# Three of the first six layer-norm passes on GpSimd instead of VectorE, and the first two weight loads released two tiles earlier

## The chip, the cores and the metric

The kernel runs on one core of one Trainium2 chip. The metric is the device time of one execution in microseconds (us). It is given as the median of several executions, and one execution is also recorded by the hardware profiler.

## What is computed

The reference is a transformer block with global attention and relative position terms, followed by a spectral layer. Everything is float32; the image has 48 x 48 = 2304 tokens of 768 channels. Cut to what matters here:

```
xn  = layernorm(x, ln1_g, ln1_b)                 # over the 768 channels of each token
qkv = xn.reshape(2304, 768) @ qkv_w + qkv_b      # 768 -> 3 x 768
q, k, v = qkv split into 12 heads of 64
attn = softmax(q * scale @ k^T + rel_h + rel_w)
x = x + (attn @ v) @ proj_w + proj_b
x = x + gelu(layernorm(x) @ mlp_w1 + b1) @ mlp_w2 + b2
x = x + irfft2(softshrink(two block layers(rfft2(x))))   # layer 1
```

The change lies in the first line of this: the layer norm of the first 768 tokens, and the loads of the first columns of qkv_w.

## The kernel before

Tokens lie on the 128 partitions of the on-chip memory, so the 2304 tokens are 18 tiles of 128. Three tiles are a group (`arrive(g)` loads them into one buffer `x3`), and two groups are a block of 768 tokens. The first stage, `queries_keys_values`, has three such blocks (`p` = 0, 1, 2). In each block, six pairs of heads give queries and keys (`queries_and_keys`), and three calls of `values` give the values.

The matrix products of this stage use Strassen's scheme in Winograd's form: seven products of half size in the place of eight. It needs sums of blocks of both operands. The sums of the tokens are made on VectorE by `sums_of_tokens` (L171, four instructions of 128x1152). The sums of the weights are made on GpSimd by `left` (L153 to L156, four instructions of 128x384 for each pair of heads), as soon as that pair's weights have landed.

Before the first product, a tile passes through these steps:

1. `arrive` asks for the tile on SP's queue (L386).
2. `normalise` (L111 to L126): two `bn_stats` (L115) and one `bn_aggr` (L117) on VectorE give mean and variance; ScalarE takes the root (L119); VectorE takes the reciprocal (L120) and then writes (x - mean) * rstd in place with one `tensor_scalar` of 128x768 (L123).
3. `channels_first` (L395 to L411) transposes the group on TensorE (L401, 18 transposes a group, in PSUM banks m0 to m3 that are used in turn). VectorE (L404) and ScalarE (L408) write the transposed tiles, scaled and shifted, to `xt`, every second channel block each.

The order in the program is: tiles 0 to 5 normalised, group 0 transposed, group 1 transposed, sums of tokens, first pair of heads.

`weights_of(pr, slot, behind)` asks for the two halves of one pair's weights on SP's queue (L362, 384 KB each). For the first two pairs the load is made to wait for an instruction, `behind`: the list `normalised` holds the last instruction of each tile's `normalise`, and the two loads wait for those of tiles 2 and 4. Then `weights_of` calls `left` on GpSimd.

The order on TensorE and on SP's queue is the order of the program text (`manual_schedule`). The order on VectorE, ScalarE and GpSimd in this stage is set by the planner of the tile framework when the kernel is built: from the instructions that are ready by its own reckoning, it takes the one that stands first in the program. The hardware then runs each engine's list strictly in that order. The statistics `stats`, `mv` and `rstd` come from a pool with three buffers each, so tile 3 uses those of tile 0, and so on.

GpSimd has, besides the sums of the weights, the additions at L612, L679, L926, L1066, L1067, L1105 and L1270, and one `tensor_scalar` with constant operands late in the kernel (L1247).

Of the kernel before, what the change touches and what calls it, by code (L numbers as in the profile page):

```python
# [13 lines left out]
ALU = mybir.AluOpType  # L14
# [30 lines left out]
def block_then_afno(  # L45
# [26 lines left out]
    nc = tc.nc  # L72
# [35 lines left out]
    xt = shared[:, : NC * TB].rearrange("p (c t) -> p c t", c=NC)  # L108
    xs = shared[:, NC * TB :].rearrange("p (k c t) -> p k c t", k=3, c=3)

    def normalise(pool, src, hat=None, made=None):  # L111

        stats = pool.tile([P, 2, 6], F32, name="stats")
        for i in range(2):
            nc.vector.bn_stats(stats[:, i, :], src[:, ts(i, C // 2)])  # L115
        mv = pool.tile([P, 2], F32, name="mv")
        nc.vector.bn_aggr(mv, stats.rearrange("p a b -> p (a b)"))  # L117
        rstd = pool.tile([P, 1], F32, name="rstd")
        nc.scalar.activation(rstd, mv[:, 1:2], AF.Sqrt, bias=eps)  # L119
        nc.vector.reciprocal(rstd, rstd)  # L120
        if hat is None:
            hat = pool.tile([P, C], F32, name="hat", bufs=4)
        last = nc.vector.tensor_scalar(hat, src, mv[:, 0:1], rstd, ALU.subtract, ALU.mult)  # L123
        if made is not None:
            made.append(last)
        return hat  # L126
# [25 lines left out]
    def left(eng, a11, a12, a21, a22, s):  # L152
        eng.tensor_tensor(s[0], a21, a22, ALU.add)  # L153
        eng.tensor_tensor(s[1], s[0], a11, ALU.subtract)  # L154
        eng.tensor_tensor(s[2], a12, s[1], ALU.subtract)
        eng.tensor_tensor(a21, a11, a21, ALU.subtract)  # L156
# [30 lines left out]
    with ExitStack() as flag_scope:  # L187
# [11 lines left out]
        with ExitStack() as att:  # L199
# [120 lines left out]
            def queries_keys_values(qkv):  # L320
# [19 lines left out]
                ln1 = qkv.enter_context(tc.tile_pool(name="ln1", bufs=3))  # L340
# [18 lines left out]
                def weights_of(pr, slot, behind=None):  # L359
                    w, ws = pairs[slot]  # L360
                    for i in range(2):
                        load = nc.sync.dma_start(  # L362
                            out=w[:, :, i],
                            in_=qkv_w[:, ds(i * C + pr * P, P)].rearrange("(c p) f -> p c f", p=P),
                        )
                        if behind is not None:
                            tc.add_manual_dep(
                                load.ins, behind.ins.name,
                                mybir.DependencyInfo(
                                    mybir.DependencyClass.Sync, mybir.DependencyReason.DATA  # L370
                                ),
                                reason="tokens first",
                            )
                    left(
                        nc.gpsimd, w[:, 0:3, 0], w[:, 3:6, 0], w[:, 0:3, 1], w[:, 3:6, 1],
                        [ws[:, i] for i in range(3)],
                    )
                    return w, ws
# [10 lines left out]
                normalised = []  # L389

                def normal(t):
                    x3 = arrived[t // 3]
                    normalise(ln1, x3[:, t % 3], x3[:, t % 3], normalised)

                def channels_first(g):  # L395
                    x3 = arrived[g]
# [96 lines left out]
                for t in range(6):  # L493
                    normal(t)
# [7 lines left out]
                    orders.append(work)  # L502

                pairs_left = [i for work in orders for kind, i in work if kind == 0]
                ahead = [weights_of(pairs_left.pop(0), i, normalised[2 + 2 * i]) for i in range(2)]
                slot = 0
                for p in range(T // TB):
                    for g in (2 * p, 2 * p + 1):
                        channels_first(g)
                    sums_of_tokens(xt, xs)  # L510
                    for n, (kind, i) in enumerate(orders[p]):
                        if kind:
                            values(p, i)
                        else:
                            queries_and_keys(p, i, *ahead.pop(0))
                            if pairs_left:
                                ahead.append(weights_of(pairs_left.pop(0), slot % 2))
                                slot += 1

                        if p == 0 and n in (3, 4):  # L520
                            weights_of_values(n - 3)
                        elif (p, n) == (0, 5):
                            constants()
                        elif p < 2 and n in (1, 2):
                            arrive(2 * p + 1 + n)
                        if p < 2 and 2 <= n < 8:
                            normal(6 * p + 4 + n)
                        if p == 2 and n == 0:
                            fetch(0)
                        elif p == 2 and n in (1, 2, 3):  # L530
                            for j in (0, 1):
                                columns(0, 2 * (n - 1) + j)
                        elif p == 2 and n in (4, 6, 8):
                            relative(0, n // 2 - 2)
                        elif p == 2 and n == 5:
                            fetch_values(0)

            with tc.manual_schedule(engines={mybir.EngineType.PE, mybir.EngineType.SP}):
                with ExitStack() as qkv:
                    queries_keys_values(qkv)  # L540
# [78 lines left out]
                with tc.manual_schedule(engines={mybir.EngineType.Activation}):  # L619
                    for n, (pr, c, u) in enumerate(runs):  # L620
# [8 lines left out]
                        made = []  # L629
# [10 lines left out]
                        if pr < NC - 1:  # L640
                            if (c, u) in ((3, 1), (4, 0), (4, 1)):
                                i = 2 * (2 * (c - 3) + u - 1)
# [89 lines left out]
        with tc.If(safe < 1):  # L732
            with ExitStack() as att:
                xnT = main.rearrange("p (c t) -> p c t", c=NC)
                with tc.tile_pool(name="g_ln1", bufs=3) as ln1, tc.tile_pool(
                    name="g_ps_ln1", bufs=2, space=PSUM
                ) as psum:
                    for g in range(T // G):
                        hats = []
                        for i in range(3):  # L740
                            xi = ln1.tile([P, C], F32, name="g_xt")
                            nc.sync.dma_start(out=xi, in_=x[ts(3 * g + i, P), :])
                            hats.append(normalise(ln1, xi))
                        transposed(psum, hats, xnT, g, V_LN1G, V_LN1B, tag="m")
# [174 lines left out]
        with tc.tile_pool(name="ps_proj", bufs=2, space=PSUM) as psum:  # L919
            hats = []  # L920
            for t in range(EARLY, NT):
                projected(psum, t, later[t] if t in later else outputs(t))
                n = t - EARLY
                if n < 6:
                    hats.append(normalise(ln2, x1[:, n, :]))
                    nc.gpsimd.tensor_tensor(x1[:, n, :], x1[:, n, :], b2, ALU.add)  # L926
                if n in (2, 5):
                    transposed(psum, hats, xt, n // 3, V_LN2G, V_LN2B, tag="t")
                    hats = []
                if n == 5:  # L930
                    sums_of_tokens(xt, xs)
# [554 lines left out]
```

## Time and profile before

| | us |
|---|---|
| median of 3 runs | 2903.45 |
| lowest and highest | 2902.31 and 2904.82 |
| profiled execution, its own time | 2902.43 |
| span of the profiled execution | 2900.4 |
| TensorE busy in the span | 2848.4 (98%) |
| VectorE busy | 1789.9 (62%) |
| ScalarE busy | 936.2 (32%) |
| GpSimd busy | 612.4 (21%) |

The span runs from the first to the last instruction of the program; the time of the execution is 2.0 us longer. Times in the profile are counted from the start of the span. TensorE was granted 0.996 of its full clock on average. Of the span, the stage that the change touches is the start: the first transpose begins at 8.17 us, and the first product of weights and tokens at 20.08 us.

### The profile page before, as it was taken

How to read it: one execution, taken by the hardware profiler on the slowest of the kernel's cores; microseconds unless marked ns; L12 is line 12 of the kernel's file. 1: busy time of each engine (PE TensorE's matmuls, PEld its weight loads, DVE VectorE, ACT ScalarE, POOL GpSimd, SP SyncE). 2: the span in 40 equal slices, each digit the busy share in tenths (PEclk: the TensorE clock that was granted, in tenths of full speed). 3: DMA queues.
4: the chain of work that ended last, by engine and by line, in shares of the span. 5: the costliest groups of instructions: out<-in, count | busy, mean ns of one | idle time of the engine just before them, and what ended most of it. 6: DMA issues, size and time to landing. Idle time of an engine off the chain costs nothing. (4 is left out here: it accounts for less than half of the span.)

```text
span 2900.4 us, 41241 instructions
## 1 busy us (share of the span) xinstructions
PE 2848.4 (98%) x15803; PEld 1703.9 (59%) x15803; DVE 1789.9 (62%) x2606; ACT 936.2 (32%) x1514; POOL 612.4 (21%) x564
## 2 busy tenths in 40 slices
PE   8999999999999999999999999999999999999998
PEld 5555665555555555555555555555555555556884
DVE  5243237777777777777733666675666666666554
ACT  1011125656566565665500210122111211112341
POOL 3303010000000000000043323333332322222441
PEclk9999999999999999999999999999999999999999
DMA  4323376172552716435252111212221212123235
GB/s 154 129 98 104 108 157 124 29 135 59 87 125 43 145 34 103 109 58 87 57 180 77 49 55 55 66 58 75 64 66 49 93 55 66 45 63 109 77 99 182
DMA packets 204595, 255.59 MB, mean 88 GB/s; under 512 B 22050, under 2 KB 182754, under 8 KB 202854
## 3 DMA queue, kind: packets, MB, share of 16 engines
q1 hardware_dynamic: 201930, 249.18, 33.5%
q10 hardware_dynamic: 2460, 3.69, 0.4%
q8 instruction: 127, 2.08, 0.3%
q14 instruction: 78, 0.64, 0.1%
HBM read 136.88 MB, written 52.20 MB: 65 GB/s over the span
## 5 line engine op out<-in xcount | busy, mean ns | idle before, releaser
L635 DVE TENSOR_TENSOR acc<-acc,main 128x768 f32<-128x768 f32 x576 | 551.8, 958 | 206.4 <-ACT main L569 149.7
L569 ACT ACTIVATE main<-sp 128x768 f32<-128x768 f32 x648 | 520.8, 812 | 138.9 <-PE sp L565 132.3
L565 PE MATMUL sp<-terms,select 64*128 64x384 f32 x1296 | 413.3, 631 | 0.0
L1051 DVE TENSOR_TENSOR main<-o,main 128x384 f32<-128x384 f32 x540 | 299.1, 556 | 38.8 <-PE o L1049 0.3
L989 PE MATMUL h<-shared,w 128*128 128x384 f32 x864 | 296.6, 486 | 0.8 <-issue 0.8
L559 PE MATMUL sp<-shared 64*128 64x384 f32 x1296 | 268.0, 490 | 2.5 <-DVE o L455 2.2
L559 PE MATMUL sp<-qT,kT 64*128 64x384 f32 x1296 | 266.7, 487 | 0.2
L612 POOL TENSOR_TENSOR inverse<-inverse,rden 128x384 f32<-128x384 f32 x36 | 46.4, 1288 | 1013.5 <-DVE rden L609 944.8
L444 PE MATMUL m<-main 128*128 128x384 f32 x756 | 246.0, 487 | 3.8 <-DVE main L171 2.9
L989 PEld LDWEIGHTS h<-shared,w 128*128 128x128 f32 x864 | 163.9, 190 | 116.3 <-issue 2.6
L989 PE MATMUL h<-shared,w1s 128*128 128x384 f32 x648 | 226.6, 486 | 0.0
L582 PE MATMUL op<-main,shared 128*64 128x384 f32 x1296 | 221.2, 488 | 0.0
L582 PE MATMUL op<-main,v 128*64 128x384 f32 x1296 | 219.9, 488 | 0.0
L995 ACT ACTIVATE hT<-c,vec 128x384 f32<-128x384 f32 x108 | 66.4, 615 | 464.9 <-DVE c L1001 464.7
L444 PEld LDWEIGHTS m<-main 128*128 128x128 f32 x756 | 142.9, 190 | 104.3 <-issue 5.0
L1001 DVE TENSOR_TENSOR c<-h,u 128x384 f32<-128x384 f32 x108 | 60.2, 557 | 212.3 <-PE h L989 212.3
L1049 PE MATMUL o<-w2s,hs 128*128 128x384 f32 x432 | 174.9, 487 | 3.2 <-DVE hs L154 3.2
L1049 PE MATMUL o<-w,hT 128*128 128x384 f32 x432 | 175.0, 487 | 3.0 <-DVE mv L117 2.0
L565 PEld LDWEIGHTS sp<-terms,select 64*128 64x128 f32 x1296 | 125.8, 187 | 84.0 <-issue 0.5
L989 PEld LDWEIGHTS h<-shared,w1s 128*128 128x128 f32 x648 | 123.1, 190 | 85.9
L153 POOL TENSOR_TENSOR w1s<-w 128x384 f32<-128x384 f32 x36 | 36.9, 1024 | 601.8 <-PE o L1049 302.1
L559 PEld LDWEIGHTS sp<-shared 64*128 64x128 f32 x1296 | 117.7, 187 | 61.4 <-issue 22.8
(158 smaller groups left out, 3860.1 us busy)
## 6 DMA issues: line engine op xcount, KB each, us to landing
w<-in_mlp_w_dram SPq DMA_DIRECT2D x72, 768.0 KB, 4.4
terms<-col_parts SPq DMA_DIRECT2D x432, 72.0 KB, 3.0
terms<-row_hi SPq DMA_DIRECT2D x216, 72.0 KB, 2.8
terms<-row_lo SPq DMA_DIRECT2D x216, 72.0 KB, 3.0
main<-in_qkv_w_dram SPq DMA_DIRECT2D x36, 384.0 KB, 4.5
z<-zt SPq DMA_DIRECT2D x48, 192.0 KB, 1.9
x<-in_x_blocks_dram SPq DMA_DIRECT2D x18, 384.0 KB, 4.6
k_d<-o SPq DMA_DIRECT2D x36, 192.0 KB, 1.8
```

Of the source, the lines that this page charges most:

```text
L444: nc.tensor.matmul(bank, a[:, c, :], b[:, c, :], start=(first and c == 0), stop=(c == 2), skip_group_check=not first,)
L559: nc.tensor.matmul(sp[:, j, :G], kT[at, ts(kt, P)], qT[at, ts(c, G)], start=True, stop=False,)
L565: nc.tensor.matmul(sp[:, j, :G], select[at, a % 2], ready[pr, c][at, a // 2, b], start=False, stop=True,)
L569: nc.scalar.activation(p, sp[:, :, :G], AF.Exp, scale=HD**-0.5)
L582: nc.tensor.matmul(op[ts(j, 64)], v[:, kt0 + i, ts(j, 64)], ps[i][:, j, :], start=(kt0 + i == 0), stop=(kt0 + i == NT - 1),)
L612: nc.gpsimd.tensor_tensor(inverse, inverse, rden, ALU.add)
L635: nc.vector.tensor_tensor(acc, made[0] if kt == 1 else acc, p, ALU.add)
L989: nc.tensor.matmul(bank[i], a[:, c, :], b[:, c, :], start=(start and c == 0), stop=(c == 2), skip_group_check=not start,)
L995: nc.scalar.activation(h[:, i, ts(k, G)], src, AF.Gelu, bias=col(V_B1 + 2 * n + i))
L1001: nc.vector.tensor_tensor(t, src, other, ALU.add)
L1049: nc.tensor.matmul(bank[k], a, b, start=start, stop=True, skip_group_check=not start)
L1051: nc.vector.tensor_tensor(dst, bank[k], dst, ALU.add)
```

## The change

In `normalise`, the engine of the last instruction becomes a parameter. For tiles 1, 3 and 5 it is GpSimd, for all others VectorE as before; statistics, root and reciprocal stay where they were. The two first weight loads wait for the last instruction of tiles 0 and 2, both of which are VectorE's, in the place of tiles 2 and 4.

```diff
-    def normalise(pool, src, hat=None, made=None):
+    def normalise(pool, src, hat=None, made=None, engine=nc.vector):
...
-        last = nc.vector.tensor_scalar(hat, src, mv[:, 0:1], rstd, ALU.subtract, ALU.mult)
+        last = engine.tensor_scalar(hat, src, mv[:, 0:1], rstd, ALU.subtract, ALU.mult)
...
                 def normal(t):
                     x3 = arrived[t // 3]
-                    normalise(ln1, x3[:, t % 3], x3[:, t % 3], normalised)
+
+                    engine = nc.gpsimd if t in (1, 3, 5) else nc.vector
+                    normalise(ln1, x3[:, t % 3], x3[:, t % 3], normalised, engine)
...
-                ahead = [weights_of(pairs_left.pop(0), i, normalised[2 + 2 * i]) for i in range(2)]
+                ahead = [weights_of(pairs_left.pop(0), i, normalised[2 * i]) for i in range(2)]
```

## The prediction

> **What bounds the kernel now.** I read the busy shares first, since they say what a saving anywhere else is worth.
>
> ```profile
> PE 2848.4 (98%) x15803; PEld 1703.9 (59%) x15803; DVE 1789.9 (62%) x2606; ACT 936.2 (32%) x1514; POOL 612.4 (21%) x564
> ```
>
> TensorE (PE) is busy for 98% of the span. So a change at the start can only move the moment from which TensorE runs without a gap; everything behind it slides along. To find that moment I took the waits of the first 30 us and then the timeline of the first 60 us (start, duration, engine, line).
>
> ```profile
> POOL main L153 <- DMA main<-in_qkv_w_dram: 14.6, 2, 14.4
> PEld m L401 <- DVE x L123: 9.8, 4, 8.2
> ```
>
> ```profile
> 7.49 1.22 DVE L123 TENSOR_SCALAR x<-x,mv,rstd 128x768 f32<-128x768 f32 x2
> ...
> 9.84 5.69 SPq L362 DMA_DIRECT2D main<-in_qkv_w_dram  x4
> ...
> 14.80 1.00 POOL L153 TENSOR_TENSOR main<-main 128x384 f32<-128x384 f32 x1 [14.36 <-DMA main<-in_qkv_w_dram]
> ...
> 15.76 0.67 DVE L123 TENSOR_SCALAR x<-x,mv,rstd 128x768 f32<-128x768 f32 x1
> ...
> 19.44 1.00 POOL L153 TENSOR_TENSOR main<-main 128x384 f32<-128x384 f32 x1 [0.24 <-DMA main<-in_qkv_w_dram]
> 19.95 7.91 DVE L171 TENSOR_TENSOR main<-main 128x1152 f32<-128x1152 f32 x4
> ...
> 20.08 2.20 PE L444 MATMUL m<-main 128*128 128x384 f32 x6 [0.44 <-DVE main L404]
> ...
> 23.86 36.45 PE L444 MATMUL m<-main 128*128 128x384 f32 x112 [1.57 <-DVE main L171]
> ```
>
> The transposes wait for VectorE's layer norm. Tile 5 is written from 15.76 to 16.43 us, its transposes (18 for group 1) and their evictions last until 20.03, the token sums start at 19.95, and their second result lets product 6 start at 23.86. From there TensorE has no gap up to 60 us. So the **start of product 6 at 23.86 us** is the number that the change can move. Back to it leads: VectorE's layer norm, tile 5's L123, the last transposes, two token sums. VectorE is full from 3.87 to 16.43 but for 0.23 us. GpSimd (POOL) is idle until 14.80.
>
> Two further rows show that VectorE and GpSimd slow each other. First, the layer norm before the MLP, where a GpSimd addition starts together with an L123 of the same shape:
>
> ```profile
> 1618.67 2.22 DVE L123 TENSOR_SCALAR hat<-main,mv,rstd 128x768 f32<-128x768 f32 x1
> ```
> ```profile
> 1618.67 1.81 POOL L1105 TENSOR_TENSOR main<-main,b 128x768 f32<-128x768 f32 x1 [46.39 <-DMA b<-in_mlp_b_dram]
> ```
>
> That L123 took 2.22 us; the same line's median in the first stage is 0.67. The second is the four token sums: 7.91 us above, beside GpSimd's sums for the second pair of weights, but 5.35 in the next block, where GpSimd is idle:
>
> ```profile
> 150.48 5.35 DVE L171 TENSOR_TENSOR main<-main 128x1152 f32<-128x1152 f32 x4
> ```
>
> **What the Trainium skill says.** "SBUF — State Buffer", section "Who interferes with whom": GpSimd and VectorE share one pair of ports. A VectorE `tensor_scalar` in its two-port mode, or a VectorE operation with two inputs in SBUF, excludes a GpSimd operation, and whichever starts first keeps the pair while the other blocks. The 2.22 us above agrees (1.81 of blocking and most of 0.67 after it). "GPSIMD Engine Reference", section 4.1: a one-input operation on GpSimd runs roughly at line rate; the trace does not agree for L1247 (below). The same page, section 2.1: the first call after a `MODIFY_POOL_CONFIG` costs about 6 us. The trace has two of these records at 0.7 to 0.8 us and two at 2641.5, ahead of L1247; in both places GpSimd goes on to wait for something else for over 13 us, so no run here shows the price.
>
> **The new instruction's cost.** No row shows a GpSimd `tensor_scalar` of 128x768 with two operands per partition. Nearest rows, by shape:
>
> ```profile
> L1247 POOL TENSOR_SCALAR o<-o 96x192 f32<-96x192 f32 x48 | 34.7, 723 | 58.0 <-ACT o L1243 31.1 <-issue 19.8 <-POOL zz L1270 7.1
> L679 POOL TENSOR_TENSOR main<-main,pb 128x768 f32<-128x768 f32 x18 | 32.5, 1846 | 3.8 <-DMA main<-in_x_dram 3.8
> ```
>
> L1247's smaller shape, 96x48, has a mean of 328 ns. Undisturbed medians are 686 (96x192), so 144 more elements cost 0.36 us, 2.5 ns each, and 768 elements come to 0.33 + 720 x 0.0025 = 2.1 us. The addition of the same shape gives 1.8. The skill's line rate, at 1.2 GHz, gives about 0.64 plus 0.2 of start, 0.9 as an estimate. I take **2.1 us**, because it is the only trend of this kind of instruction, and keep 0.9 and 2.6 as ends.
>
> **The change, part by part** (against the profiled execution, span 2900.4, time 2902.43).
>
> (1) VectorE loses three L123: tile 1 (0.57 us from start to start), tile 3 (0.58), tile 5 (0.67, the last). Free of everything else, the chain would be 1.15 us earlier at tile 5's statistics and shorter by 0.67.
>
> (2) GpSimd gains three. Tile 1: its reciprocal is there at about 7.45, tile 0's L123 holds the ports until 8.12, so it runs 8.12 to 10.2. VectorE's tile 2 would be ready at 8.6 and now blocks until 10.2, ending at 10.85 where it ended at 9.81. VectorE loses 1.0 of what part 1 gained.
>
> (3) Tile 3 on GpSimd: reciprocal at about 12.2 (11.21 before, plus that 1.0), runs 12.4 to 14.5. VectorE's tile 4, ready at about 13.9 to 14.0, blocks until 14.5 and ends at 15.15 (14.54 before). The three evictions L404 and the last reciprocal follow: the reciprocal of tile 5 comes at about 15.8 (15.12 before).
>
> (4) Tile 5 on GpSimd: 15.9 to 18.0, in the place of 15.76 to 16.43. That is **+1.57 us** for the tile that the last transposes wait for. Its 0.67 on VectorE hid nothing, so the longer 2.1 is on the path whole.
>
> (5) From tile 5's end the same 3.6 us follow (transposes and evictions, 16.43 to 20.03), then 3.8 to the second token sum. Product 6 starts near 25.4.
>
> (6) Weights. SP's queue waits for tile 0 (8.12) where it waited for tile 2 (9.81), then for tile 2 where it waited for tile 4 (14.54). Nothing else stands behind them on SP until the first store at 30.68, so these waits hold up nobody. The token tiles have landed by about 9 us (the DMA engines move 301 GB/s in the slice from 7.5 to 9.0 and 2 GB/s in the next), so the loads meet no other traffic. Four issues of some 0.5 us, landing 4.5 us after: first pair at 12.8 to 13 (14.6 before), second at 15.5 (19.3 before). TensorE waits for neither: product 6 is held by the token sum, and the second pair comes at 37 us. Their gain can only be that GpSimd is done before the token sums begin: two sums would cost 2.7 in the place of 3.8, **-1.1 us**. But GpSimd has, from 12.4, two `tensor_scalar` (4.2) and eight sums (8.0), until 24.6; the token sums start at 21.5. So in the likeliest case this gain is nearly lost: -0.1.
>
> Sum: +1.57 - 0.1 = **+1.5**, so 2903.9 for a profiled execution like this one, 1.0 below the median's 2903.45 + 1.5 = **2904.9**. For a measurement of this kernel about 0.2%, 5.8 us, can be told from no change; this is well inside.
>
> **Rivals.**
>
> (A) The likeliest, as above: a slower layer norm tile on GpSimd, +0.5 to +2.5 with 1.4 to 2.6 us per instruction. Chance 0.48.
>
> (B) GpSimd is quick (0.9). Tile 2 then blocks until 9.0 only, VectorE keeps its 1.15, tile 5 is done near 15.4 (1.0 earlier), and GpSimd is done with the weights by about 21.7, so that one token sum or both run free (-0.3 to -1.1). Sum -1.3 to -2.5: 2901 to 2902. For it: the skill's line rate; VectorE's queue is the bound. Against it: L1247's trend, and the 2.22 us row. Chance 0.31. The most that the start can give: transposes from 8.17 at their pace of 0.21 us (36 take 7.5), 1.9 for product 1 and 2.7 for two free token sums: 18.5 at the earliest, 5.3 us before 23.86. Over 5.8 faster is thus not to be had here; 0.03 remains for another order on VectorE or ScalarE later.
>
> (C) In between: some of the first pair's sums stand on GpSimd ahead of tile 5, since those weights are there from 13 and tile 5 only at 15.9. Each costs 1.0 us, so two to four give +3.5 to +5.5. Or the load of the instruction's code after `MODIFY_POOL_CONFIG` is late: 0.8 + 6 = 6.8 just fits before tile 1 at 7.45, and at the worst that the trace allows (14.8) tiles 1, 3 and 5 run back to back and end at 21.1, +4.7. Chance 0.10.
>
> (D) Slower by over 5.8: GpSimd's list has all eight weight sums ahead of tile 5. They run 13 to 21, tile 5 21 to 23.1, 6.7 us later than before: 2910. It decides from six sums ahead (tile 5's end past 22.2). Against it: tile 5 stands first in the program. Chance 0.08.
>
> The change cannot fail to act: both edits bind engine and waits directly.
>
> **Numbers.** Faster 0.03, slower 0.09 (D, and 0.01 for another order later), same 0.88. Range 2900.0 (B, less 1.1 for the runs' scatter) to 2909.0 (C's end).
>
> **What would show it.** Right: L123 on POOL near 2.1 us; VectorE's tile 2 over 1.5 us; tile 5 ending near 18.0; L444's second piece at about 25.4. Wrong: POOL's L123 under 1.2 and that piece before 23.5 (B), L153 to L156 ahead of tile 5's L123 on POOL (C, D), a POOL L123 that starts long after its reciprocal with nothing in front (the code load). If TensorE's gaps after 60 us differ, the order elsewhere has changed and the argument fails.

## The result, and the profile after

Over 20 runs of each, the changed kernel has a median of 2907.18 us and the kernel before one of 2901.78: 5.4 us longer, a ratio of 1.0019 with a 95% interval of 1.0014 to 1.0025. That is a slowdown, just under the 0.2% that the prediction counts as no change. The profiled execution of the changed kernel took 2911.11 us (span 2909.1). It lies at the upper end of its 20 runs, so its own difference, 8.7, is not taken for the effect.

The busy shares on the page of the changed kernel show no work added to TensorE:

```profile
PE 2847.6 (98%) x15803; PEld 1703.8 (59%) x15803; DVE 1785.4 (61%) x2603; ACT 935.2 (32%) x1514; POOL 617.0 (21%) x567
```

VectorE has three instructions fewer and GpSimd three more. The waits of the first 30 us (who waited for whom: total, times and longest, in us) show what TensorE waits for. Lines from the diff on are two higher than before, so the transposes are L403 now:

```profile
PE m L403 <- POOL x L123: 8.7, 2, 6.4
PE m L403 <- DVE x L123: 8.2, 1, 8.2
```

Of these, the 8.2 is the wait for the first tile, as before. The 8.7 is new, and most of it is one wait of 6.4 us. The timeline of the first 60 us of the changed kernel shows which:

```profile
7.56 0.63 DVE L123 TENSOR_SCALAR x<-x,mv,rstd 128x768 f32<-128x768 f32 x1
7.64 3.36 POOL L123 TENSOR_SCALAR x<-x,mv,rstd 128x768 f32<-128x768 f32 x1 [7.20 <-DVE mv L117]
...
8.30 1.15 DVE L123 TENSOR_SCALAR x<-x,mv,rstd 128x768 f32<-128x768 f32 x1
...
12.42 0.67 ACT L410 ACTIVATE main<-m,vec 128x384 f32<-128x384 f32 x1 [4.44 <-PE m L403]
12.99 0.28 ACT L119 ACTIVATE rstd<-mv,eps 128x1 f32<-128x1 f32 x1
13.30 0.17 DVE L120 RECIPROCAL rstd<-rstd 128x1 f32<-128x1 f32 x1 [0.85 <-ACT rstd L119]
...
13.57 3.01 POOL L123 TENSOR_SCALAR x<-x,mv,rstd 128x768 f32<-128x768 f32 x1 [2.58 <-DVE rstd L120]
...
15.24 0.67 DVE L123 TENSOR_SCALAR x<-x,mv,rstd 128x768 f32<-128x768 f32 x1
...
16.48 0.15 DVE L120 RECIPROCAL rstd<-rstd 128x1 f32<-128x1 f32 x1
16.56 0.99 POOL L153 TENSOR_TENSOR main<-main 128x384 f32<-128x384 f32 x1
...
19.53 0.99 POOL L155 TENSOR_TENSOR main<-main 128x384 f32<-128x384 f32 x1
20.50 2.93 POOL L123 TENSOR_SCALAR x<-x,mv,rstd 128x768 f32<-128x768 f32 x1
...
27.15 5.45 DVE L171 TENSOR_TENSOR main<-main 128x1152 f32<-128x1152 f32 x4
...
30.12 30.26 PE L446 MATMUL m<-main 128*128 128x384 f32 x93 [0.50 <-DVE main L171]
```

Read it from the end. The seven products are made in the order 1, 6, 7, 5, 2, 4, 3, so product 6 is the second, and the first that needs a sum of tokens. It starts at 30.12 in the place of 23.86, **6.26 us later**. Back from there:

- The token sums start at 27.15 (19.95 before), and product 6 starts 2.97 after them (3.91 before): 0.94 is won. GpSimd has nearly finished the second pair's weights by then, and the four sums take 5.45 in the place of 7.91.
- Tile 5 ends at 23.43 (20.50 + 2.93) in the place of 16.43: **7.00 later**. From its end to the token sums it is 3.72 in the place of 3.52, another 0.20.

So 7.00 + 0.20 - 0.94 = 6.26. Tile 5's 7.00 has three parts. Its reciprocal ends at 16.63 in the place of 15.27 (+1.36). From there to the start of L123 it is 3.87 in the place of 0.49 (+3.38): the four weight sums of the first pair, L153 at 16.56 being the first and L155 at 19.53 the last, stand ahead of it on GpSimd. L123 itself takes 2.93 in the place of 0.67 (+2.26). This is an account in time and not a list of causes: even with the reciprocal as early as before, tile 5 could not have started sooner, since GpSimd was at tile 3 until 16.58 and then at the four sums.

Two later marks show what becomes of the 6.26. The first matmul of the attention scores (L559 before, L561 after) starts at 423.0 in the place of 417.0, and the first of the projection (L692 and L694) at 1470.5 in the place of 1464.5: still 6.0. So TensorE's gaps up to there hardly change the sum, which the prediction had named as a condition. The rest of the profiled 8.7 arises behind that. In e2 below, with the same three tiles, the projection starts at 1470.9, 6.4 later than before, and yet its profiled span is only 2.4 longer (2902.8). What comes behind 1470 us thus differs by several us from one execution to the next, and is not put down to the change.

### The profile page after: what moved, and what is told of

It reads as the page before. It is cut to its first block, busy times and chain, and to the rows that moved or that the text cites. A ratio compares the mean times of both kernels' runs of the same rounds, so it can differ in the third digit from the quotient of the medians.

```text
span 2909.1 us, 41244 instructions
## 1 busy us (share of the span) xinstructions
PE 2847.6 (98%) x15803; PEld 1703.8 (59%) x15803; DVE 1785.4 (61%) x2603; ACT 935.2 (32%) x1514; POOL 617.0 (21%) x567
## 5 line engine op out<-in xcount | busy, mean ns | idle before, releaser
L561 PE MATMUL sp<-shared 64*128 64x384 f32 x1296 | 268.1, 490 | 2.5 <-DVE o L457 2.2
L561 PE MATMUL sp<-qT,kT 64*128 64x384 f32 x1296 | 266.2, 488 | 0.2
L153 POOL TENSOR_TENSOR w1s<-w 128x384 f32<-128x384 f32 x36 | 36.6, 1018 | 603.2 <-PE o L1051 336.2
L561 PEld LDWEIGHTS sp<-shared 64*128 64x128 f32 x1296 | 117.8, 187 | 61.3 <-issue 23.1
```

What stands on the lines that cost most here:

```text
L561: nc.tensor.matmul(sp[:, j, :G], kT[at, ts(kt, P)], qT[at, ts(c, G)], start=True, stop=False,)
```

## The experiments

"Product 6" is the start of that product, found as above in each run's timeline. "Scores" is the start of the first matmul of the attention scores, which come behind this stage. The ratio is the time against that of the kernel before. Edits of e4, e5 and e10 move the lines: in e5 and e10 the token sums (L171) are L172, and the products (L444 before) are L455 in e5.

| run | product 6, us | scores, us | ratio, 95% interval |
|---|---|---|---|
| before | 23.86 | 417.0 | |
| the change | 30.12 | 423.0 | 1.0019, 1.0014 to 1.0025 |
| e1 loads earlier, all tiles on VectorE | 24.21 | 416.5 | 0.9998, 0.9990 to 1.0007 |
| e2 tiles on GpSimd, loads as before | 30.17 | 423.4 | 1.0018, 1.0010 to 1.0027 |
| e3 the change, GpSimd in program order | 27.51 | 425.3 | 1.0026, 1.0016 to 1.0037 |
| e4 tiles on ScalarE, loads earlier | 23.90 | 417.0 | 0.9998, 0.9990 to 1.0006 |
| e5 the change, tile 5 ahead of the weight sums | 27.09 | 420.5 | 1.0009, 1.0002 to 1.0016 |
| e6 tile 1 alone on GpSimd | 26.42 | 419.0 | 1.0005, 0.9996 to 1.0013 |
| e7 tile 5 alone on GpSimd | 28.06 | 422.5 | 1.0013, 1.0006 to 1.0019 |
| e9 tile 3 alone on GpSimd | 23.94 | 416.6 | 0.9995, 0.9987 to 1.0004 |
| e10 as e9, second pair's sums after the token sums | 22.93 | 416.6 | 0.9995, 0.9986 to 1.0003 |

A step of 0.0001 is 0.29 us. Apart from e3, the time follows product 6 within its interval in every row. The shift of the scores also holds what happens between product 6 and them; it differs from the shift of product 6 by 4.6 us in e3 and by up to 1.3 in the other rows.

**e1, the earlier loads alone**

```diff
-                    engine = nc.gpsimd if t in (1, 3, 5) else nc.vector
+                    engine = nc.vector
```

> The loads of the first two pairs wait for tiles 0 and 2 as in the change, but all six tiles stay on VectorE. Theory Q (the lateness comes from tile 5 on GpSimd, three sizes too slow and behind four weight sums in GpSimd's queue): the loads are harmless, GpSimd is done with both pairs by about 21 us, the token sums run nearly free, product 6 starts near 23.0 in the place of 23.86, and the time is 0.5 to 1.0 us below before. Rival W (the earlier loads disturb the token loads or the queue): product 6 starts later than 23.86 and a good part of the 5.4 us is here.

Measured: median 2901.48 against 2902.08, no difference that shows. Product 6 starts at 24.21, not at 23.0: this part of theory Q is a miss. The weights do come sooner: the first pair's sums start at 13.28 on GpSimd, in the place of 14.80. But now they run beside VectorE's layer norm. The timeline of e1:

```profile
13.79 0.90 DVE L123 TENSOR_SCALAR x<-x,mv,rstd 128x768 f32<-128x768 f32 x1
...
24.21 1.21 PE L446 MATMUL m<-main 128*128 128x384 f32 x3 [1.23 <-DVE main L171]
```

Tile 4's L123 takes 0.90 and tile 5's 1.00, both 0.67 before. The token sums start 0.69 later (20.64), and win back half of it since only one of the weight sums is still beside them (5.96 for the four). What the loads win at one end is paid at the other. Rival W has product 6 on its side, but its main point falls: no good part of the 5.4 us is here.

**e2, GpSimd alone**

```diff
-                ahead = [weights_of(pairs_left.pop(0), i, normalised[2 * i]) for i in range(2)]
+                ahead = [weights_of(pairs_left.pop(0), i, normalised[2 + 2 * i]) for i in range(2)]
```

> Tiles 1, 3 and 5 on GpSimd as in the change, the loads wait for tiles 2 and 4 as before. Theory Q: the first pair's weights still land by about 14.5 us, before GpSimd is done with tile 3 at 16.6, and the planner's order on GpSimd is the same, so product 6 starts at 30 us as in the change and the time is 5 to 6 us above before. Rival W: less than half of that.

Measured: median 2907.80, ratio 1.0018, as theory Q has it. The timeline of e2:

```profile
20.55 2.93 POOL L123 TENSOR_SCALAR x<-x,mv,rstd 128x768 f32<-128x768 f32 x1
```

Tile 5 starts at 20.55 against 20.50 in the change. GpSimd is busy with tile 3 until 16.6, and the weights wait for it, whenever they were asked for. The slowdown comes from the three tiles; no part of it by the loads shows. The 0.94 won at the token sums is in e2 as well (5.5 for the four), so it is not the loads' doing either.

**e3, tile 5 first by the program's order**

```diff
-                with ExitStack() as qkv:
+                with ExitStack() as qkv, tc.manual_schedule(engines={mybir.EngineType.Pool}):
                     queries_keys_values(qkv)
```

> The whole change, and GpSimd keeps the order of the program in the first stage, so that tile 5 stands ahead of the first pair's four weight sums. Theory Q: tile 5 runs from 16.6 to 19.5 in the place of 20.5 to 23.4; GpSimd then makes the weight sums beside the token sums, which cost 3.8 in the place of 2.7 up to the second; product 6 starts near 27 in the place of 30.1, and the time is 2 to 3 us above before. Rival P (VectorE loses by sharing its ports, whatever the order on GpSimd): no better than the change, 5 to 6 us above before.

Measured: median 2908.49, ratio 1.0026: a miss in time, though product 6 starts at 27.51 as expected. The waits of TensorE in e3 have a line that the change has only with 0.4 us:

```profile
PE m L477 <- POOL wv L156: 3.1, 1, 3.1
```

The program's order also puts L155 ahead of L156 for the value weights, where the planner has them the other way round, and TensorE's first products of values wait 3.1 us for L156. The 3.65 at the start and most of that 3.1 make 6 to 7, and by the scores it is 8.3; the ratio says 7.5, with an interval of 4.6 to 10.7. So e3 changed two things, and e5 repeats the question.

**e5, tile 5 first by a dependency alone**

```diff
+                    if behind is not None:
+                        tc.add_manual_dep(first.ins, normalised[5].ins.name, ...)
```

Here `first` is the first instruction of `left` for that pair.

> The whole change; only the first weight sum of each of the first two pairs is made to wait for tile 5 on GpSimd, and the rest of GpSimd's order is the planner's. It repeats the question of e3 without what e3 also moved (the sums of the value weights, for which TensorE waited 3.1 us there). Theory Q: tile 5 ends at about 19.5, the token sums run beside the weight sums, product 6 starts near 27, and the time is 2.5 to 4 us above before. Rival P (it is not tile 5's place in GpSimd's queue that costs): 5 to 6 us above before, as in the change.

Measured: median 2904.31 against 2901.97, ratio 1.0009. The timeline of e5:

```profile
16.78 2.93 POOL L123 TENSOR_SCALAR x<-x,mv,rstd 128x768 f32<-128x768 f32 x1 [0.15 <-DVE rstd L120]
...
27.09 4.20 PE L455 MATMUL m<-main 128*128 128x384 f32 x12 [1.30 <-DVE main L172]
```

Tile 5 runs right behind its reciprocal and ends 3.7 us sooner than in the change. Of that, 0.7 is given back at the token sums, which now run beside the weight sums (7.65 for the four). So about half of the slowdown was tile 5's place in the queue: 3.0 of the 6.3 at product 6 and 2.5 of the 6.0 at the scores. In time it is 2.9 of 5.4, but the intervals of the two ratios just touch. The other half stays, 3.2 at product 6: tile 5's reciprocal is 1.4 later than in the kernel before, and its instruction takes 2.26 more and starts 0.4 sooner behind that reciprocal.

**e6 and e7, one tile alone**

```diff
-                    engine = nc.gpsimd if t in (1, 3, 5) else nc.vector
+                    engine = nc.gpsimd if t in (1,) else nc.vector     # e6; (5,) in e7; loads as before
```

> Only tile 1 goes to GpSimd, loads as before. Theory Q with the second part of it, theory S (tile 1 ends near 11.1, so the first transposes do too; ScalarE's list has the eviction of a transpose ahead of the root of tile 3, which waits with it, and tile 3's reciprocal comes at 13.3 in the place of 11.2): tile 5 is done on VectorE near 17.8 in the place of 16.4, product 6 starts near 25, and the time is 1 to 1.5 us above before. Rival H (tile 1 on GpSimd is hidden behind VectorE's other work, and VectorE is 0.57 us earlier): product 6 near 23.3 and the time 0 to 0.6 us below before.

> Only tile 5 goes to GpSimd, loads as before. Theory Q: the planner again puts the first pair's four weight sums ahead of it; they start when the weights land, at about 14.8, and end at 18.8, tile 5 takes 2.9 and ends near 21.7 in the place of 16.4; the second pair's sums come later beside the token sums; product 6 starts at 28 to 29 and the time is 4 to 5 us above before. Rival P: the loss needs tiles 1 and 3 too, and the time is 1 to 2 us above before.

e7 came as expected at product 6 (28.06); the median is 2906.05 and the ratio 1.0013, 3.8 us above before where 4 to 5 were expected, which its interval holds. The timeline of e7 has the queue plainly, the last of four weight sums and tile 5 behind it:

```profile
17.47 0.99 POOL L155 TENSOR_TENSOR main<-main 128x384 f32<-128x384 f32 x1
18.45 2.93 POOL L123 TENSOR_SCALAR x<-x,mv,rstd 128x768 f32<-128x768 f32 x1
```

Its reciprocal was there at 15.24. So tile 5 alone makes most of the change's cost: two thirds at product 6 and in time, and 5.5 of 6.0 at the scores. What tiles 1 and 3 add at product 6, 2.06, is that GpSimd comes to the weight sums later: tile 5 starts 2.05 later in the change than here.

e6 speaks against rival H, but in the profile only: tile 1 ends at 11.25, tile 3's reciprocal comes at 13.55 behind ScalarE's eviction, tile 5 ends at 18.34 and product 6 starts at 26.42. The time, 1.0005, is within its interval of both no change and +2.6, so it decides nothing. Product 6 is 1.4 later than expected, 0.5 of it at the end of tile 5, whose L123 took 1.00 in the place of 0.67 beside a weight sum, and the rest behind it, half of that at the token sums: the weights, released by tiles that were themselves late, kept GpSimd busy beside the first three of the four (7.54 in all).

**e8, the instruction by itself**

```diff
+                    if t == 12:
+                        nc.gpsimd.tensor_scalar(a, a, 1.0, None, ALU.mult)
...
+                    elif t == 15:
+                        nc.gpsimd.tensor_scalar(a, a, zero, one, ALU.subtract, ALU.mult)
```

> The kernel before, with one more GpSimd tensor_scalar in place on each of tiles 12 to 16, ahead of their layer norm; it subtracts 0, multiplies by 1 or both, so that nothing changes in the result. Forms: tile 12 one constant, 13 two constants, 14 one operand per partition, 15 two operands per partition, 16 the same on half the tile (128x384). Theory V (operands per partition make GpSimd slow): 12 and 13 at 2.1 us, 14 and 15 near 2.9. Rival O (the second operation makes it slow): 12 and 14 near 2.1, 13 and 15 near 2.9. Rival N (neither; the trend of the small shapes was no guide): all of 12 to 15 near 2.9. Tile 16 near 1.5 in each case.

The timeline of e8 around tiles 12 to 16, GpSimd only:

```profile
185.10 2.14 POOL L396 TENSOR_SCALAR x<-x 128x768 f32<-128x768 f32 x1 [68.59 <-DVE u L438]
187.19 2.80 POOL L398 TENSOR_SCALAR x<-x 128x768 f32<-128x768 f32 x1
189.97 2.40 POOL L400 TENSOR_SCALAR x<-x,ones 128x768 f32<-128x768 f32 x1
...
200.87 2.94 POOL L402 TENSOR_SCALAR x<-x,inverse,ones 128x768 f32<-128x768 f32 x1 [8.50 <-DMA x<-in_x_blocks_dram]
203.78 1.65 POOL L404 TENSOR_SCALAR x<-x,inverse,ones 128x384 f32<-128x384 f32 x1
```

There is one instruction of each form, in one execution. In order: one constant 2.14, two constants 2.80, one operand per partition 2.40, two of them 2.94, half the tile 1.65. Rival O is the nearest: the second operation costs 0.54 to 0.66 us, operands per partition in the place of constants only 0.14 to 0.26. Neither theory V nor N fits. That the cost belongs to this form and not to the start of the kernel is shown as well: two operands per partition take 2.94 here and 2.93 for tile 5 in the change.

**e4, ScalarE in GpSimd's place**

```diff
+        if engine is nc.scalar:
+            nc.vector.scalar_tensor_tensor(shift, mv[:, 0:1], -1.0, rstd, ALU.mult, ALU.mult)
+            last = nc.scalar.activation(hat, src, AF.Identity, bias=shift, scale=rstd)
```

> Tiles 1, 3 and 5 are written by ScalarE (identity with scale rstd and bias -mean*rstd, which VectorE makes with one more 128x1 instruction a tile), the loads wait as in the change. Theory Q: a tile costs ScalarE some 0.8 us, VectorE keeps most of the 1.7 us that it saves, product 6 starts between 22 and 23.5, the time is 0.5 to 2 us below before. Rival: ScalarE's evictions of transposes are pushed back by the tiles and eat the gain, 0 to 1 us above before.

Measured: median 2900.94 against 2902.08, ratio 0.9998: no difference that shows. Theory Q's 22 to 23.5 for product 6 is missed (23.90). A tile costs ScalarE 1.03 us, not 0.8, and tile 5 ends at 16.65, 0.2 later than before. ScalarE is no remedy for the start, but as an engine for these tiles it costs nothing that shows, where GpSimd costs 5.4.

**e9 and e10, a tile with slack**

```diff
+                    engine = nc.gpsimd if t in (3,) else nc.vector     # both
...
+                    if sums is not None:                               # e10: sums is the last token sum
+                        tc.add_manual_dep(first.ins, sums.ins.name, ...)
```

In e10 the second pair's `weights_of` also moves behind the token sums in the program; its loads still go out as in e9.

> Only tile 3 goes to GpSimd, loads as before. Theory K (a tile on GpSimd is free where it has 3 us of slack before TensorE asks for it): tile 3 runs from 11.4 to 14.4, its transposes are wanted at about 15.5, the planner leaves ScalarE's order as before, VectorE is 0.6 us shorter, product 6 starts between 23.0 and 23.6, and the time is the same as before or up to 1 us below. Rival P (any tile on GpSimd costs VectorE more in shared ports than it saves): product 6 after 24.2 and the time 1 us or more above before.

> As e9, and GpSimd's weight sums of the second pair wait for the last token sum (they are needed only near 36 us). Theory K with the shared ports at the token sums: these take 5.4 us in the place of 7.9, product 6 starts between 21.9 and 22.6, and the time is 1 to 2 us below before, which five rounds may just tell from no change. Rival (the second pair's sums, started near 24.5 and done near 28.5, come too late or hinder VectorE's sums behind them): product 6 as early, but a wait of TensorE near 36 us, and the time as before.

e9: tile 3 runs from 11.52 to 14.46 and is wanted at 15.66, so it is hidden; tile 5 ends 0.3 sooner. But product 6 starts at 23.94, because the token sums, started at 19.82, meet the weight sums (8.12 for the four). Theory K is right on tile 3 and wrong on what follows, and neither its range nor rival P's holds 23.94. e10 takes that away:

```profile
20.16 5.35 DVE L172 TENSOR_TENSOR main<-main 128x1152 f32<-128x1152 f32 x4
```

Product 6 starts at 22.93, 0.9 sooner than before and 0.3 later than expected, and TensorE has no wait near 36 us. At the scores 0.4 of the 0.9 is left. The medians are 2900.64 and 2899.54 against 2901.04. Both intervals hold no change, so it is not shown that either beats the kernel before; both beat the changed kernel.

## Why the prediction was right or wrong

**The range held by luck.** 2907.18 lies within 2900.0 to 2909.0, but not by the argument that was put first: case A ended at +2.5, and the change cost 5.4. The range reached that far for case C, which had a chance of 0.10. Even C's price fits for a part by accident. It took 1.0 us for each sum ahead of tile 5 and 2.1 for the tile; with four sums tile 5 came 7.00 late, more than C's upper end of 5.5, and the token sums gave 0.94 back.

**Right:** the place, and the sign of the likeliest case. Product 6 is the number that the change moves first, tile 5 is the tile on the path (e7), and the earlier loads win nothing that shows (e1, e2). That the start alone could not give 5.8 us was not put to a test; the most that a run won there is 0.9 (e10). The 18.5 that the prediction gives as the earliest start is 8.17 and 7.5 for the transposes and 2.7 for two token sums; the 1.9 for product 1 that stands in the same list runs beside the sums and is not in it. The load of instruction code after `MODIFY_POOL_CONFIG` was no obstacle: the records are at 0.7 to 0.8 us and tile 1 starts at 7.64, directly behind its reciprocal.

**Wrong, step (4), and with it the choice between A and C.** The sum put tile 5 at 15.9 to 18.0 with nothing ahead of it. It ran from 20.50 behind four weight sums: this is case C. The argument used against D, that tile 5 stands first in the program, fails: the list that the planner made has the four sums first. That it reckoned those weights ready before tile 5 is inferred from its rule; no run shows the reckoning. C and D also let the first pair's sums start at 13, though by step (3) GpSimd is at tile 3 until 14.5; they started at 16.56, behind tile 3. e5 prices the place in the queue at 3.0 us at product 6 (30.12 less 27.09) and about 2.9 of time (1.0019 less 1.0009, with the wide interval named there).

**Wrong, the cost of the instruction.** 2.1 us, with 2.6 as the upper end; measured 3.36, 3.01 and 2.93. The row it came from, L1247, has one operation with a constant. e8 shows that its trend was right for that form (2.14 at 128x768), and that the new instruction's second operation and its operands per partition add 0.8. The term was mis-sized because the row was taken by engine and shape and not by the number of operations.

**Wrong, step (2), the blocking.** The step let tile 2 on VectorE wait for tile 1's end and finish at 10.85. It took 1.15 and ended at 9.45, while GpSimd's L123 went on until 11.00. Step (3) expected a wait for tile 4 and there was none (0.67 at 15.24, inside GpSimd's 13.57 to 16.58). The exclusion that the Trainium skill states ("SBUF — State Buffer", section "Who interferes with whom") agrees with the GpSimd addition at 1618.67 in the kernel before, but does not describe these two pairs: VectorE's instruction started second and ended first.

Something of it is left, though. In e9 tile 4's L123 on VectorE took 0.93:

```profile
11.52 2.94 POOL L123 TENSOR_SCALAR x<-x,mv,rstd 128x768 f32<-128x768 f32 x1 [11.08 <-DVE rstd L120]
...
13.95 0.93 DVE L123 TENSOR_SCALAR x<-x,mv,rstd 128x768 f32<-128x768 f32 x1
```

GpSimd ended its tile at 14.46 and began a weight sum at 14.62, and either can have held VectorE up. GpSimd's 3.36 for tile 1 is open as well: tile 0's L123 ran on VectorE beside its first 0.55 us, tile 2's beside a later part. In every run that has tile 1 on GpSimd, both were there, so no run tells which of them made it 0.43 longer than tile 5's 2.93.

**Missed: ScalarE.** Step (3) had tile 3's reciprocal at 12.2, late by VectorE's blocking. It came at 13.30, for another reason: ScalarE's list now has the eviction L410 (12.42, the copy of a transposed block out of PSUM) ahead of the root of tile 3 (12.99). The eviction waits for the transposes, and these for tile 1 on GpSimd. In the kernel before, the root came first:

```profile
10.88 0.29 ACT L119 ACTIVATE rstd<-mv,eps 128x1 f32<-128x1 f32 x1 [2.98 <-DVE mv L117]
11.08 0.65 ACT L408 ACTIVATE main<-m,vec 128x384 f32<-128x384 f32 x1
11.21 0.16 DVE L120 RECIPROCAL rstd<-rstd 128x1 f32<-128x1 f32 x1
```

e6 shows the late reciprocal with tile 1 alone on GpSimd (13.55), and in e9, with tile 1 on VectorE, it comes at 11.24.

**Step (6), too small and for another reason.** The gain of 0.1 at the token sums was 0.94, but only because the sums came so late that GpSimd had nearly done the weights while TensorE stood idle for tile 5. Since e2 has the same 0.94, the earlier loads did not make it.

## What to carry to other kernels

Before an instruction is moved to another engine, look at what that engine's queue holds at that moment: a tile that is last on the path must not stand behind work that is needed later, and where a planner sets the order, a dependency has to say so. Price the instruction by a row with the same number of operations, not by engine and size alone. And a helper engine hides a tile only where that has more slack than the helper takes (tile 3 here, and not tile 5); that this wins time was not shown here (e9, e10).

## What the hardware showed that was not expected

The time of a `tensor_scalar` on GpSimd depends on how many operations it has: 2.14 us with one and 2.80 with two, at the same 128x768 and with constants (e8). And two `tensor_scalar` of that size on GpSimd and VectorE did not exclude each other: VectorE's took 0.67 inside GpSimd's at 15.24 in the change and 0.66 at 191.02 in e8, and 1.15 at 8.30 and 0.93 in e9, but in each of the first three cases it ended while GpSimd's was still running. The GpSimd addition at 1618.67, which started together with VectorE's and took 1.81, made that 2.22. Why it is sometimes 0.67 and sometimes more stays open.
